# Rotation issued in three steps, and the next batch's normalized sequence in two halves scaled by GpSimd, in a transformer layer on one core

## The chip, the core and the metric

The kernel runs on one core of a Trainium2 chip. The metric is the device time of one execution in microseconds (us), lower is better. The engines are named as the profile names them: PE is TensorE (PEld its weight loads), DVE is VectorE, ACT is ScalarE, POOL is GpSimd, and SP is SyncE, whose queue issues the DMAs of this kernel. Each engine runs its own instructions in the order in which they were issued, and waits for others through semaphores.

## The reference

Four sequences of 1024 tokens with 1024 features, float32. Attention has 32 heads of 32 features, and the feed-forward part sends each token to the best of eight low-rank adapters.

```python
# x: (4, 1024, 1024); layernorm has no weights, eps = 1e-5
x = x + attn(layernorm(x), wq, wk, wv, wo)
x = x + ffn(layernorm(x), route_w, A, Bw)

def attn(x, ...):                        # H, HD = 32, 32
    q, k, v = x @ wq, x @ wk, x @ wv     # each split into heads
    q, k = rotary(q), rotary(k)          # pairs of features: x0*cos - x1*sin, x0*sin + x1*cos
    probs = softmax(causal(q @ k.T / sqrt(HD)))
    return (probs @ v) @ wo

def ffn(x, ...):                         # E, R = 8, 16
    logits = x @ route_w.T               # the best expert, weighted by its logit
    wh = one_hot(argmax(logits)) * max(logits) * (x @ A.T)
    return wh @ Bw                       # summed over experts and ranks
```

## The kernel before

**Units.** The work is cut into 32 units (b, g): four batches b of eight groups g of four heads, whose 4 x 32 features fill the 128 partitions. A unit computes scores, softmax and values for its four heads. The scores come in rounds in the fixed order SLOTS: pieces named by the block t of 64 queries (t = 0 to 15, block t has (t + 1) x 64 keys, so a query row of score data has (t + 1) x 32 elements per partition) are computed in the order 7 and 6; 5, 4 and 3; then "second"; 2, 1, 0 and 9; 15; 14; 13; 12; then "first"; 11 with a part of 8; 10 with the rest. "first" multiplies the probabilities of this unit's first half of the queries by the values, "second" those of the second half of the unit before.

**A round.** `score_round` has PE write the scores into the tile `s` (L381), the only buffer of its PSUM pool; ACT copies them to SBUF (`pr`, L392); POOL adds the causal mask on the diagonal block (L395). `find_tops` has DVE take the row maxima (`top`, L413) and join two partition groups (`both`, L434). Later ACT exponentiates (L442), and DVE transposes (L467). `apply` multiplies with the values (`av`, L548) into the same PSUM tile as the scores, and DVE scales the product by the reciprocal sums and so empties the tile (`scale_values`, L568). The reciprocal sums are spread by a POOL copy (`by`, L512), transposed by PE (L522) and copied by ACT (L523).

**Steps between the rounds.** The rest of the work is a list of `Step` objects for each unit, `between[u]`, each with a cost. After every round `fill` takes steps off the list in order, until their costs reach the round's share of what is left. So the program's order is written once, when it is built, and every step's instructions join their engines' queues at that point. For a unit u the list holds the projections of unit u + 1, by `chain`: q, k and v, each for the two halves `tb` of the sequence, eight matmuls of 128x512 a chain (L295). From batch 1 on it also has the output projection of the batch before, `po` with its streamed weight `chunk` (L665), and that tile's norm, routing and adapter.

**Rotation.** `chain` ends in `finish`. For q and k, ACT copies PSUM to `raw` (L321, L323), DVE shuffles neighbouring partitions into `other` (named swapq or swapk, L325), POOL multiplies `raw` by the cosines in place (L326), DVE multiplies `other` by the signed sines (L327), and POOL adds both into `qT` or `kT` (L328). All five are issued at once. Since L326 writes `raw`, which the shuffle reads, it waits for the shuffle. `raw` and `other` share three buffers of the tag rope.

**The first norm.** Class `Norm` brings the eight tiles of 128 tokens of a batch into `xnT`, the normalized and transposed sequence. `load` reads a tile (L127; some tiles are kept in the next unit's `qT` and `kT`, L246, by the table `homes`). `find` takes moments (`find_moments`: DVE L175, L177 and L179, then POOL raises to the power -0.5, L181). `scale` normalizes in place by one DVE instruction (L186); before it scales tile t it finds the moments of tile t + 1. `turn` transposes by PE in two banks `pt_a` (L198), and copies them to `xnT`, the first bank by ACT (L200), the second by DVE (L204), or by ACT in batch 0. `xnT` is one tile of 128 x 8 x 1024 with one buffer, so no tile of the next batch can be turned before the last v chain of the present batch has read it. `change_steps` and `begin_steps` write the list of steps of the unit in which batches change: the output projection's steps with turnings 0 to 3 among them, then the q and k chains woven with turnings 4 to 7. From batch 0 to 1 there is no output projection, so turnings 0 to 3 stand at the front of the list. The next batch's x tiles share four `row` buffers with the residual tiles; SP issues their loads in order with the weight chunks, the values' round trip through DRAM and the stores.

**Masks behind rotations.** POOL's queue holds masks, rotation products and sums, the powers and the copies of L512, in the order of issue.

Of the kernel before, what the change touches and what calls it, by code (L numbers as in the profile page):

```python
# [9 lines left out]
F32 = mybir.dt.float32  # L10
AF = mybir.ActivationFunctionType
ALU = mybir.AluOpType
AX = mybir.AxisListType

P = 128
# [42 lines left out]
def weave(main, other):  # L58

    if not other:  # L60
        return list(main)
    out, taken = [], 0
    for n, step in enumerate(main):
        out.append(step)
        due = (n + 1) * len(other) // len(main)
        out += other[taken:due]
        taken = due
    return out + list(other[taken:])
# [3 lines left out]
def tile_preln_attn_then_top1_lora(  # L72
# [17 lines left out]
    nc = tc.nc  # L90
# [7 lines left out]
    NC = D // P  # L98
# [6 lines left out]

    const = ctx.enter_context(tc.tile_pool(name="const", bufs=1))
    big = ctx.enter_context(tc.tile_pool(name="big", bufs=1))
    COUNT = {"row": 4, "w": 2, "qkT": 4, "rope": 3, "vT": 1, "vals": 1}
    small = ctx.enter_context(tc.tile_pool(name="small", bufs=2))
    dram = ctx.enter_context(tc.tile_pool(name="dram", bufs=2, space=bass.MemoryType.DRAM))  # L110
    ps_s = ctx.enter_context(tc.tile_pool(name="ps_s", bufs=1, space=bass.MemoryType.PSUM))
# [69 lines left out]
        nc.gpsimd.tensor_tensor(rstd, ve, half_sb, ALU.pow)  # L181
        return mv, rstd

    def normalize(dst, src, moments):
        mv, rstd = moments
        nc.vector.tensor_scalar(dst, src, mv[:, 0:1], rstd, ALU.subtract, ALU.mult)  # L186

    def layernorm(dst, src, name):
        normalize(dst, src, find_moments(src, name))
# [30 lines left out]

    xnTs, qTs, kTs, vTs = {}, {}, {}, {}

    class Norm:


# [28 lines left out]
        def scale(self, t):  # L254
            while self.scaled <= t:
                k = self.scaled
                self.find(k + 1)
                normalize(self.x[k], self.x[k], self.moments.pop(k))
                self.scaled += 1

        def turn(self, t):
            if t == 0:
                xnTs[self.b] = big.tile([P, NC, S], F32, tag="xnT", name=f"xnT_{self.b}")
            self.scale(t)
            dst = xnTs[self.b][:, :, t * P : (t + 1) * P]
            transposed(dst, self.x.pop(t), f"a{self.b}_{t}", scalar_only=not self.b)
            self.load(*self.after.get(t, ()))

        def scaling(self, t):
            return Step(lambda: self.scale(t), 0.0)  # L270

        def turning(self, t):
            return Step(lambda: self.turn(t), 2.0)

        def steps(self, tiles):

# [7 lines left out]
    def chain(u, n, tb, parts=False):  # L284


        b = units[u][0]
        cols = slice(tb * HALF, (tb + 1) * HALF)
        at = {}

        def step(c):
            if c == 0:
                at["p"] = bank([P, HALF], f"p{n}_{u}_{tb}")
            wt = weights[u, n]
            nc.tensor.matmul(  # L295
                at["p"],
                lhsT=wt[:, c, :],
                rhs=xnTs[b][:, c, cols],
                start=(c == 0),
                stop=(c == NC - 1),  # L300
            )
            if c == NC - 1:
                finish()

        def finish():
            if tb == 1:
                weights.pop((u, n))
                if (u, n) != (0, "v"):
                    load_weights()
            if n == "v":  # L310
                if tb == 0:
                    vTs[u] = big.tile([P, S], F32, tag="vT", name=f"vT_{u}")
                nc.scalar.copy(vTs[u][:, cols], at["p"])
                return
            dsts = qTs if n == "q" else kTs
            if u not in dsts:
                dsts[u] = big.tile([P, S], F32, tag="qkT", name=f"{n}T_{u}", bufs=4)
            dst = dsts[u]
            raw = big.tile([P, HALF], F32, tag="rope", name=f"raw{n}_{u}_{tb}", bufs=3)
            if n == "q":  # L320
                nc.scalar.mul(raw, at["p"], scale)  # L321
            else:
                nc.scalar.copy(raw, at["p"])  # L323
            other = big.tile([P, HALF], F32, tag="rope", name=f"swap{n}_{u}_{tb}", bufs=3)
            nc.vector.stream_shuffle(other, raw, SWAP)  # L325
            nc.gpsimd.tensor_tensor(raw, raw, cos_sb[:, cols], ALU.mult)  # L326
            nc.vector.tensor_tensor(other, other, sin_sb[:, cols], ALU.mult)  # L327
            nc.gpsimd.tensor_tensor(dst[:, cols], raw, other, ALU.add)  # L328

        def part(t):  # L330

            if t == 0:
                at["p"] = bank([P, HALF], f"p{n}_{u}_{tb}")
            wt = weights[u, n]
            for c in range(NC):
                nc.tensor.matmul(
                    at["p"][:, t * P : (t + 1) * P],
                    lhsT=wt[:, c, :],
                    rhs=xnTs[b][:, c, t * P : (t + 1) * P],
                    start=(c == 0),  # L340
                    stop=(c == NC - 1),
                )
            if t == TB - 1:
                finish()

        if parts:
            return [Step(lambda t=t: part(t), 2.0) for t in range(TB)]
        return [Step(lambda c=c: step(c)) for c in range(NC)]
# [241 lines left out]

    def load_wo():

        wt = big.tile([P, NC, D], F32, tag="xnT", name="wo_all")
        wo_all.append(wt)
        for n in range(2):
            cols = slice(n * 512, (n + 1) * 512)
            for c in range(NC):
                nc.sync.dma_start(wt[:, c, cols], wo[c * P : (c + 1) * P, cols])

    kept = {}  # L600

# [29 lines left out]
    def finish_steps(b, t, kind="stream"):  # L631
# [22 lines left out]
        def project(n, c, k=None, start=None, stop=None):  # L654
            if c == start:
                st["po"] = bank([P, 512], f"po_{name}_{n}_{start}")
            if k is None:
                rhs = wo_all[0][:, c, n * 512 : (n + 1) * 512]
            else:
                rhs = take_chunk(k)  # L660
            if c < far:
                lhsT = st["at"][:, c, :]
            else:
                lhsT = last_attn[t // TB][:, (t % TB) * P : (t % TB + 1) * P]
            nc.tensor.matmul(st["po"], lhsT=lhsT, rhs=rhs, start=(c == start), stop=(c == stop))  # L665
            if k is not None:
                load_chunk(k + 4)
            if c == stop:
                y = st["y"]
                cols = slice(n * 512, (n + 1) * 512)  # L670
                nc.vector.tensor_tensor(y[:, cols], st["po"], y[:, cols], ALU.add)
                if n == 1 and stop == NC - 1:
                    st["yn"] = kept[t - TB] if last and t >= TB else row(f"yn_{name}")
                    layernorm(st["yn"], y, f"f{name}")
# [85 lines left out]
        return Step(fetch, 0.0), chains, tail  # L760


    def begin_steps(u, norm, project_end):

        q0k0 = chain(u, "q", 0) + chain(u, "k", 0)
        out = [norm.scaling(TB)] + weave(q0k0[:13], norm.steps(range(TB, NT))) + project_end + q0k0[13:]
        for n, tb in (("q", 1), ("k", 1), ("v", 0), ("v", 1)):
            out += chain(u, n, tb)
        return out

    def change_steps(u, norm, project, tail):


        turn, route, turn_hidden, adapt = tail
        p, turning, scaling = project, norm.turning, norm.scaling
        out = [*p[:3], turn, *p[3:5], route, *p[5:8], turn_hidden, *p[8:11], adapt]
        out += [Step(lambda: norm.load(2, 5), 0.0), scaling(1), *p[11:13], turning(0), scaling(2)]
        out += [turning(1), scaling(3), *p[13:15], turning(2), turning(3)]
        return out + begin_steps(u, norm, p[15:])

    norms = {}
    between, late_fetch = [], {}
# [1 line left out]
    for u, (b, g) in enumerate(units):  # L784
# [10 lines left out]


        if u + 1 < len(units) and g + 1 == NG:
            if b:
                homes = {0: "q", 1: "k", 3: "q", 4: "k"}
                norm = Norm(b + 1, {0: (3,), 1: (4,), 2: (6,), 5: (7,)}, homes)  # L800
                steps = change_steps(u + 1, norm, project, tail)
            else:
                norm = Norm(b + 1, {0: (5,), 1: (6,), 2: (7,)}, {4: "k"})
                for t in reversed(range(TB)):
                    between[-1].insert(16 + 8 * t, norm.scaling(t))
                between[-1].insert(0, Step(lambda norm=norm: norm.load(*range(TB)), 0.0))
                steps = [norm.turning(t) for t in range(TB)] + begin_steps(u + 1, norm, [])
            norms[b + 1] = norm
        else:
            steps = []  # L810
# [74 lines left out]
    def do(s):  # L885
        if s.chunk:
            s.run(numbers[s])
        else:
            s.run()

    for s in start:
        do(s)
# [43 lines left out]
    second, first_ = SLOTS.index("second"), SLOTS.index("first")  # L936
    final = len(units) - 1
    for u, (b, g) in enumerate(units):
        todo.extend(between[u])
        ends_at = n_slots  # L940
        if b + 1 < B and g + 1 == NG:
            norms[b + 1].load(*((0, 1) if b else (TB,)))
        if u == final:
            load_wo()
            ends_at = second
# [121 lines left out]
```

## Time and profile before

| | |
|---|---|
| median of the three runs | 2840.68 us (2840.13, 2840.68, 2847.22) |
| the profiled execution | 2841.66 us |
| its span, first to last instruction | 2839.9 us |
| mean granted clock of PE | 0.983 |
| row maxima, L413, DVE | 652.1 us in 768 instructions |
| causal masks, L395, POOL | 238.5 us in 512 instructions |
| rotation products of k, L326, POOL | 114.1 us in 64 instructions |
| normalization of one tile, L186, DVE | 0.80 us, up to 1.50 |
| second copy of a turned tile, DVE L204 / ACT L200 | 0.69 / 0.59 us |

Busy times come from one profiled execution. In a row of the timeline the columns are start, busy time, engine, line, operation, output and inputs, tile and number of instructions, and in brackets the idle time of the engine before it and what ended that. A count such as x5 means that neighbouring instructions of one kind are drawn together, with the tile of one of them. In a row of the windows each engine's busy us in the stretch is followed by its number of instructions; then come PE's granted clock, the busy share of the DMA engines and GB/s. In a row of the waits the numbers are the us in total, how often, and the longest.

### The profile page before, as it was taken

How to read it: one execution, taken by the hardware profiler on the slowest of the kernel's cores; microseconds unless marked ns; L12 is line 12 of the kernel's file. 1: busy time of each engine (PE TensorE's matmuls, PEld its weight loads, DVE VectorE, ACT ScalarE, POOL GpSimd, SP SyncE). 2: the span in 40 equal slices, each digit the busy share in tenths (PEclk: the TensorE clock that was granted, in tenths of full speed). 3: DMA queues.
4: the chain of work that ended last, by engine and by line, in shares of the span. 5: the costliest groups of instructions: out<-in, count | busy, mean ns of one | idle time of the engine just before them, and what ended most of it. 6: DMA issues, size and time to landing. Idle time of an engine off the chain costs nothing.

```text
span 2839.9 us, 84110 instructions
## 1 busy us (share of the span) xinstructions
PE 2713.1 (96%) x35328; PEld 1334.1 (47%) x35328; DVE 2119.5 (75%) x4225; ACT 1746.1 (61%) x5006; POOL 711.7 (25%) x900
## 2 busy tenths in 40 slices
PE   8999999889999999988999999998999999999998
PEld 5444444344444444443445544444444445444445
DVE  4777777887777777787777787777777777877655
ACT  2776777676667666655666666664666666676421
POOL 2322222323222222212222222221222222222000
PEclk9999999999999999999999999999999999999999
DMA  3222222223544544562454445545164444445521
GB/s 114 50 54 54 54 51 51 82 72 85 141 125 134 143 133 127 135 191 50 117 157 117 122 124 145 140 128 177 46 168 121 139 124 115 127 135 146 168 65 53
DMA packets 448011, 317.86 MB, mean 112 GB/s; under 512 B 150288, under 2 KB 371728, under 8 KB 447632
## 3 DMA queue, kind: packets, MB, share of 16 engines
q1 hardware_dynamic: 447632, 312.47, 40.0%
q8 instruction: 278, 4.55, 0.7%
q14 instruction: 101, 0.83, 0.1%
HBM read 262.59 MB, written 49.81 MB: 110 GB/s over the span
## 4 chain that ended last, share of the span: by engine, by line
PE 81%; DVE 10%; POOL 3%; DMA 2%; ACT 2%; issue 1%; SPq 0%; POOLq 0%; DVEq 0%; ACTq 0%
PE po L665 14%; PE pq L295 14%; PE pv L295 13%; PE pk L295 13%; PE s L381 12%; PE av L548 8%; DVE top L413 4%; DVE pr L467 2%; PE ph L686 2%; PE pf L725 2%; PE pr L522 1%; DVE both L434 1%; DMA chunk<-in_wo 1%; PE pt_f L198 1%; POOL pr L395 1%
## 5 line engine op out<-in xcount | busy, mean ns | idle before, releaser
L442 ACT ACTIVATE pr<-pr,both 128x256 f32<-128x256 f32 (+15 forms) x2048 | 1047.1, 520 | 40.4 <-DVE both L434 39.6
L413 DVE TENSOR_REDUCE top<-pr 128x2 f32<-128x960 f32 (+15 forms) x768 | 652.1, 896 | 354.4 <-POOL pr L395 353.1
L392 ACT COPY pr<-s 128x640 f32<-128x640 f32 (+14 forms) x544 | 525.9, 1018 | 563.5 <-PE s L381 563.3
L467 DVE STREAM_TRANSPOSE pr<-pr 128x1024 f32<-128x1024 f32 (+11 forms) x768 | 671.4, 910 | 51.2 <-ACT pr L442 47.3
L395 POOL TENSOR_TENSOR pr<-pr,causal_sb 128x128 f32<-128x128 f32 x512 | 238.5, 472 | 1054.2 <-ACT pr L392 1045.4
L295 PE MATMUL pv<-xnT,wv 128*128 128x512 f32 x1024 | 489.5, 607 | 0.0
L295 PE MATMUL pq<-xnT,wq 128*128 128x512 f32 x1008 | 483.3, 607 | 3.2 <-ACT xnT L200 3.2
L295 PE MATMUL pk<-xnT,wk 128*128 128x512 f32 x1008 | 474.8, 601 | 1.5 <-ACT rawq L321 1.5
L381 PE MATMUL s<-kT,qT 32*32 32x256 f32 (+4 forms) x17408 | 403.3, 395 | 48.7 <-DVE at L568 47.1
L442 ACT ACTIVATION_READ_ACCUMULATOR pr<-pr,both 128x1 f32 x2048 | 402.6, 197 | 0.0
L665 PE MATMUL po<-chunk,attn 128*128 128x512 f32 x736 | 377.5, 600 | 7.2 <-DMA chunk<-in_wo 7.2
L381 PEld LDWEIGHTS s<-kT,qT 32*32 32x32 f32 x17408 | 190.9, 104 | 306.9 <-issue 174.8
L295 PEld LDWEIGHTS pv<-xnT,wv 128*128 128x128 f32 x1024 | 189.1, 193 | 223.8 <-issue 219.0
L295 PEld LDWEIGHTS pq<-xnT,wq 128*128 128x128 f32 x1008 | 184.8, 193 | 232.5 <-issue 228.1
L295 PEld LDWEIGHTS pk<-xnT,wk 128*128 128x128 f32 x1008 | 182.1, 190 | 236.9 <-issue 234.0
L548 PE MATMUL av<-pr,vals 64*32 64x256 f32 (+3 forms) x12288 | 269.2, 318 | 4.2 <-issue 2.1
L548 PEld LDWEIGHTS av<-pr,vals 64*32 64x32 f32 x12288 | 212.2, 105 | 110.7 <-issue 28.7
L665 PEld LDWEIGHTS po<-chunk,attn 128*128 128x128 f32 x736 | 135.1, 190 | 174.7 <-issue 150.7
L434 DVE TENSOR_TENSOR both<-top 32x4 f32<-32x4 f32 (+3 forms) x1152 | 187.3, 163 | 23.7
L523 ACT COPY by<-pr 128x512 f32<-128x512 f32 x64 | 37.5, 586 | 260.8 <-PE pr L522 260.8
L326 POOL TENSOR_TENSOR rawk<-rawk,cos_sb 128x512 f32<-128x512 f32 x64 | 114.1, 1784 | 289.0 <-DVE swapk L325 289.0
L326 POOL TENSOR_TENSOR rawq<-rawq,cos_sb 128x512 f32<-128x512 f32 x64 | 114.1, 1782 | 246.4 <-DVE swapq L325 246.4
(88 smaller groups left out, 1723.8 us busy)
## 6 DMA issues: line engine op xcount, KB each, us to landing
chunk<-in_wo SPq DMA_DIRECT2D x368, 256.0 KB, 3.8
vals<-vd SPq DMA_DIRECT2D x256, 128.0 KB, 4.4
x<-in_x SPq DMA_DIRECT2D x55, 512.0 KB, 5.8
wq<-in_wq SPq DMA_DIRECT2D x32, 512.0 KB, 4.1
wk<-in_wk SPq DMA_DIRECT2D x32, 512.0 KB, 4.2
wv<-in_wv SPq DMA_DIRECT2D x32, 512.0 KB, 4.2
vd<-vT SPq DMA_DIRECT2D x128, 128.0 KB, 4.8
out_y<-x SPq DMA_DIRECT2D x32, 512.0 KB, 2.8
```

The lines of the kernel that those rows point to most:

```text
L295: nc.tensor.matmul(at["p"], lhsT=wt[:, c, :], rhs=xnTs[b][:, c, cols], start=(c == 0), stop=(c == NC - 1),)
L326: nc.gpsimd.tensor_tensor(raw, raw, cos_sb[:, cols], ALU.mult)
L381: nc.tensor.matmul(sc[i * SQ : (i + 1) * SQ, h, at : at + w].rearrange("p (j k) -> p j k", k=SQ), lhsT=of_q[rows, 2 * t + half], rhs=of_k[ ...
L392: nc.scalar.copy(pr[:, :, k0 : k0 + w], sc[:, :, at : at + w])
L395: nc.gpsimd.tensor_tensor(diagonal, diagonal, causal_sb.unsqueeze(1).to_broadcast([P, HG, SQ]), ALU.add)
L413: nc.vector.tensor_reduce(top[:, k, h : h + step], places[u, t][:, h : h + step, :], AX.X, ALU.max, negate=True,)
L434: nc.vector.tensor_tensor(dst[rows], src[rows], src[other], op)
L442: nc.scalar.activation(pr[:, h, :], pr[:, h, :], AF.Exp, bias=tops[u, t][:, h : h + 1], accum_out=dens[u, t // QT][:, t % QT, h : h + 1],)
L467: nc.vector.transpose(pr, pr)
L548: nc.tensor.matmul(avs[half][h * HD : (h + 1) * HD, t0:, :], lhsT=v[rows, j, h * HD : (h + 1) * HD], rhs=rhs, start=(j == 0), stop=(j == n ...
L665: nc.tensor.matmul(st["po"], lhsT=lhsT, rhs=rhs, start=(c == start), stop=(c == stop))
L686: nc.tensor.matmul(ph, lhsT=st["ynT"][:, c, :], rhs=w[:, c - i * RA, :], start=(c == 0), stop=(c == NC - 1),)
```

## The change

1. The rotation is taken apart. `finish` makes only the raw copy. A list `postponed` with `do_postponed` runs after every step and counts its cost: after two units of cost the shuffle, the product (which now writes `qT` or `kT` and leaves `raw` alone) and the sine product are issued, after two more the sum, now in place in `qT` or `kT`. Whatever is left is issued at the start of a unit.
2. `xnT` becomes two halves of 128 x 8 x 512 in two buffers. The first half's buffer is free after the last v chain of that half. Turnings of the next batch's first tiles (0 to 3 from batch 0 to 1, tile 0 in the later changes) move among the last steps of the list before, that is among the last v chain, and the output weights for the last batch are two tiles for the same reason.
3. In batches 1 to 3 `normalize` runs on POOL, two `tensor_scalar` of 128x512 for a tile in place of one of 128x1024 on DVE (48 in place of 24), and both copies of a turned tile are ACT's in all batches (24 ACT copies in place of 24 on DVE). A turning costs 1.3 instead of 2.0 in the lists of batches 1 to 3.
4. The tag row has five buffers instead of four, x tiles are loaded earlier and in other homes, and `change_steps` sets another order of chains and turnings, in the change from batch 0 too; `begin_steps` is gone.

```diff
--- before.py
+++ after.py
...
     big = ctx.enter_context(tc.tile_pool(name="big", bufs=1))
-    COUNT = {"row": 4, "w": 2, "qkT": 4, "rope": 3, "vT": 1, "vals": 1}
+    COUNT = {"row": 5, "w": 2, "qkT": 4, "rope": 3, "vT": 1, "vals": 1}
     small = ctx.enter_context(tc.tile_pool(name="small", bufs=2))
...
 
-    def normalize(dst, src, moments):
+    def normalize(dst, src, moments, engine=None):
         mv, rstd = moments
-        nc.vector.tensor_scalar(dst, src, mv[:, 0:1], rstd, ALU.subtract, ALU.mult)
+        if engine is None:
+            nc.vector.tensor_scalar(dst, src, mv[:, 0:1], rstd, ALU.subtract, ALU.mult)
+            return
+        for n in range(D // 512):
+            cols = slice(n * 512, (n + 1) * 512)
+            engine.tensor_scalar(dst[:, cols], src[:, cols], mv[:, 0:1], rstd, ALU.subtract, ALU.mult)
 
...
 
+
+    postponed = []
+
+    def do_postponed(cost):
+        for item in list(postponed):
+            item[0] -= cost
+            if item[0] <= 0:
+                postponed.remove(item)
+                item[1]()
+
     class Norm:
...
                 self.find(k + 1)
-                normalize(self.x[k], self.x[k], self.moments.pop(k))
+                engine = nc.gpsimd if self.b else None
+                normalize(self.x[k], self.x[k], self.moments.pop(k), engine)
                 self.scaled += 1
 
         def turn(self, t):
-            if t == 0:
-                xnTs[self.b] = big.tile([P, NC, S], F32, tag="xnT", name=f"xnT_{self.b}")
+            half, k = divmod(t, TB)
+            if k == 0:
+                xnTs[self.b, half] = big.tile(
+                    [P, NC, HALF], F32, tag="xnT", name=f"xnT_{self.b}_{half}", bufs=2
+                )
             self.scale(t)
-            dst = xnTs[self.b][:, :, t * P : (t + 1) * P]
-            transposed(dst, self.x.pop(t), f"a{self.b}_{t}", scalar_only=not self.b)
+            dst = xnTs[self.b, half][:, :, k * P : (k + 1) * P]
+            transposed(dst, self.x.pop(t), f"a{self.b}_{t}", scalar_only=True)
             self.load(*self.after.get(t, ()))
 
         def scaling(self, t):
             return Step(lambda: self.scale(t), 0.0)
 
         def turning(self, t):
-            return Step(lambda: self.turn(t), 2.0)
+            return Step(lambda: self.turn(t), 2.0 if self.b == 0 else 1.3)
 
...
                 lhsT=wt[:, c, :],
-                rhs=xnTs[b][:, c, cols],
+                rhs=xnTs[b, tb][:, c, :],
                 start=(c == 0),
...
                 nc.scalar.copy(raw, at["p"])
-            other = big.tile([P, HALF], F32, tag="rope", name=f"swap{n}_{u}_{tb}", bufs=3)
-            nc.vector.stream_shuffle(other, raw, SWAP)
-            nc.gpsimd.tensor_tensor(raw, raw, cos_sb[:, cols], ALU.mult)
-            nc.vector.tensor_tensor(other, other, sin_sb[:, cols], ALU.mult)
-            nc.gpsimd.tensor_tensor(dst[:, cols], raw, other, ALU.add)
+
+            def turn():
+                other = big.tile([P, HALF], F32, tag="rope", name=f"swap{n}_{u}_{tb}", bufs=3)
+                nc.vector.stream_shuffle(other, raw, SWAP)
+                nc.gpsimd.tensor_tensor(dst[:, cols], raw, cos_sb[:, cols], ALU.mult)
+                nc.vector.tensor_tensor(other, other, sin_sb[:, cols], ALU.mult)
+                postponed.append([2.0, lambda: add(other)])
+
+            def add(other):
+                nc.gpsimd.tensor_tensor(dst[:, cols], dst[:, cols], other, ALU.add)
+
+            postponed.append([2.0, turn])
 
...
 
-    def begin_steps(u, norm, project_end):
-
-        q0k0 = chain(u, "q", 0) + chain(u, "k", 0)
-        out = [norm.scaling(TB)] + weave(q0k0[:13], norm.steps(range(TB, NT))) + project_end + q0k0[13:]
-        for n, tb in (("q", 1), ("k", 1), ("v", 0), ("v", 1)):
-            out += chain(u, n, tb)
-        return out
-
     def change_steps(u, norm, project, tail):
 
 
-        turn, route, turn_hidden, adapt = tail
         p, turning, scaling = project, norm.turning, norm.scaling
-        out = [*p[:3], turn, *p[3:5], route, *p[5:8], turn_hidden, *p[8:11], adapt]
-        out += [Step(lambda: norm.load(2, 5), 0.0), scaling(1), *p[11:13], turning(0), scaling(2)]
-        out += [turning(1), scaling(3), *p[13:15], turning(2), turning(3)]
-        return out + begin_steps(u, norm, p[15:])
+        out, chains = [], []
+        for n, tb in (("q", 0), ("k", 0), ("q", 1), ("k", 1), ("v", 0), ("v", 1)):
+            chains += chain(u, n, tb)
+        if p:
+            turn, route, turn_hidden, adapt = tail
+            out += [*p[:2], scaling(1), turn, *p[2:4], turning(1), route, scaling(2), *p[4:6], turning(2)]
+            out += [turn_hidden, scaling(3), p[6], adapt, Step(lambda: norm.load(7), 0.0)]
+            out += [turning(3), scaling(4), p[7]]
+            chains = weave(chains[:-6], p[8:]) + chains[-6:]
+        else:
+            out += [scaling(4)]
+        for t, n in zip(range(TB, NT), (3, 4, 5, 4)):
+            out += chains[:n] + [turning(t)] + [scaling(t + 1)] * (t + 1 < NT)
+            del chains[:n]
+        return out + chains
 
...
         if u + 1 < len(units) and g + 1 == NG:
+            last_v = between[-1]
             if b:
-                homes = {0: "q", 1: "k", 3: "q", 4: "k"}
-                norm = Norm(b + 1, {0: (3,), 1: (4,), 2: (6,), 5: (7,)}, homes)
-                steps = change_steps(u + 1, norm, project, tail)
+                norm = Norm(b + 1, {0: (1,), 1: (4,), 2: (5,), 3: (6,)}, {2: "q", 3: "k", 5: "q", 6: "k"})
+                last_v.insert(len(last_v) - 6, norm.turning(0))
+                last_v.insert(len(last_v) - 15, norm.scaling(0))
+                last_v.insert(len(last_v) - 24, Step(lambda norm=norm: norm.load(0), 0.0))
             else:
-                norm = Norm(b + 1, {0: (5,), 1: (6,), 2: (7,)}, {4: "k"})
+                norm = Norm(b + 1, {0: (5,), 1: (6,), 2: (7,)})
                 for t in reversed(range(TB)):
-                    between[-1].insert(16 + 8 * t, norm.scaling(t))
-                between[-1].insert(0, Step(lambda norm=norm: norm.load(*range(TB)), 0.0))
-                steps = [norm.turning(t) for t in range(TB)] + begin_steps(u + 1, norm, [])
+                    last_v.insert(len(last_v) - 7 + 2 * t, norm.turning(t))
+                for t in reversed(range(TB)):
+                    last_v.insert(12 + 7 * t, norm.scaling(t))
+                last_v.insert(0, Step(lambda norm=norm: norm.load(*range(TB + 1)), 0.0))
+            steps = change_steps(u + 1, norm, project, tail)
             norms[b + 1] = norm
...
             s.run()
+        do_postponed(s.cost)
 
...
     for u, (b, g) in enumerate(units):
+        do_postponed(math.inf)
+        do_postponed(math.inf)
         todo.extend(between[u])
         ends_at = n_slots
         if b + 1 < B and g + 1 == NG:
-            norms[b + 1].load(*((0, 1) if b else (TB,)))
+            if b:
+                norms[b + 1].load(2, 3)
         if u == final:
```

More of the change, by code (lines that the diff above doesn't have):

```diff
@@ L338, in part @@
                     lhsT=wt[:, c, :],
-                    rhs=xnTs[b][:, c, t * P : (t + 1) * P],
+                    rhs=xnTs[b, tb][:, c, t * P : (t + 1) * P],
                     start=(c == 0),
@@ L591, in load_wo @@
     def load_wo():
-        wt = big.tile([P, NC, D], F32, tag="xnT", name="wo_all")
-        wo_all.append(wt)
         for n in range(2):
             cols = slice(n * 512, (n + 1) * 512)
+            wt = big.tile([P, NC, 512], F32, tag="xnT", name=f"wo_{n}", bufs=2)
+            wo_all.append(wt)
             for c in range(NC):
-                nc.sync.dma_start(wt[:, c, cols], wo[c * P : (c + 1) * P, cols])
+                nc.sync.dma_start(wt[:, c, :], wo[c * P : (c + 1) * P, cols])
     kept = {}
@@ L657, in project @@
             if k is None:
-                rhs = wo_all[0][:, c, n * 512 : (n + 1) * 512]
+                rhs = wo_all[n][:, c, :]
             else:
```

## The prediction

> **What bounds the kernel now.** I read the page's first part, then the chain that ended last, then a table of windows, then TensorE's (PE's) waits, and last the timeline of one repeated unit of work. From the page:
>
> ```profile
> span 2839.9 us, 84110 instructions
> PE 2713.1 (96%) x35328; PEld 1334.1 (47%) x35328; DVE 2119.5 (75%) x4225; ACT 1746.1 (61%) x5006; POOL 711.7 (25%) x900
> ...
> PE 81%; DVE 10%; POOL 3%; DMA 2%; ACT 2%; issue 1%; SPq 0%; POOLq 0%; DVEq 0%; ACTq 0%
> ```
>
> PE is busy for 96%, so only 127 us of the span can be idle. The change takes no matmul away; it can win only that idle time and the cold clock after it. The windows (us, then busy us by engine, then granted clock) show where it is:
>
> ```profile
> 351.00:423.00 72.00, 65.87 (x1034) 31.14 (x1032) 56.73 (x112) 53.04 (x155) 20.54 (x26) 0.95 0.22 53
> 495.00:576.00 81.00, 67.70 (x1055) 32.38 (x1065) 67.30 (x133) 53.32 (x156) 23.96 (x30) 0.92 0.27 73
> 576.00:662.00 86.00, 76.27 (x1128) 39.26 (x1097) 71.67 (x141) 57.82 (x164) 24.03 (x30) 0.94 0.25 69
> 801.00:890.00 89.00, 89.00 (x1236) 44.35 (x1236) 69.70 (x140) 56.91 (x164) 24.54 (x29) 1.00 0.46 128
> 1239.00:1308.00 69.00, 49.58 (x680) 26.71 (x679) 53.39 (x112) 30.54 (x102) 14.74 (x20) 0.94 0.57 158
> ```
>
> A unit inside batches 1 to 3 (801) has PE full at clock 1.00. A unit of batch 0 (351) lacks 6 us, the two units around the change from batch 0 to 1 (495, 576) 13 and 10, and a later change of batch (1239) 19. PE's waits say on what:
>
> ```profile
> PE s L381 <- DVE at L568: 47.1, 8, 11.2
> PE pt_a L198 <- DVE x L186: 29.1, 7, 9.3
> PE pt_a L198 <- DVE kT L186: 7.2, 2, 3.9
> PE pt_a L198 <- DVE qT L186: 6.9, 4, 2.3
> ```
>
> The first is a score round that waits for VectorE (DVE) to empty the shared PSUM tile (L568); the others are transposes of a tile of x that wait for its normalization. The timeline of one batch-0 unit (start, us, engine, operation, idle before and its releaser) shows how DVE comes to be late:
>
> ```profile
> 377.31 1.79 POOL L326 TENSOR_TENSOR rawk<-rawk,cos_sb 128x512 f32<-128x512 f32 x1 [6.70 <-DVE swapk L325]
> 379.18 1.27 POOL L328 TENSOR_TENSOR kT<-rawk,swapk 128x512 f32<-128x512 f32 x1
> 380.42 1.70 POOL L395 TENSOR_TENSOR pr<-pr,causal_sb 128x128 f32<-128x128 f32 x4
> 380.90 2.80 DVE L413 TENSOR_REDUCE top<-pr 128x4 f32<-128x384 f32 x5 [1.32 <-POOL pr L395]
> 389.11 1.79 POOL L326 TENSOR_TENSOR rawq<-rawq,cos_sb 128x512 f32<-128x512 f32 x1 [4.54 <-DVE swapq L325]
> 390.98 1.28 POOL L328 TENSOR_TENSOR qT<-rawq,swapq 128x512 f32<-128x512 f32 x1
> 392.21 0.46 POOL L395 TENSOR_TENSOR pr<-pr,causal_sb 128x128 f32<-128x128 f32 x1
> 392.71 2.21 DVE L413 TENSOR_REDUCE top<-pr 128x2 f32<-128x960 f32 x2 [2.13 <-POOL pr L395]
> 412.65 2.37 PE L381 MATMUL s<-kT,qT 32*32 32x384 f32 x64 [6.13 <-DVE at L568]
> ```
>
> GpSimd (POOL) runs in order: a rotation's product waits for DVE's shuffle, its sum follows, and the causal masks queue behind both; the row maxima (top) wait for the masks; after further DVE work stands L568, for which PE waits 6.13 us.
>
> **Rotation apart, in batch 0.** The shuffle moves some steps behind the raw copy, the product writes qT or kT and so no longer waits for the shuffle, and the sum comes a step later. No instruction is added. I follow a unit by the rows: the score copy of round 14 ended at 390.31, so its mask could end at about 390.8 if the sum did not stand in front (the product, 1.79, can start at 387.7, when the raw copy ends). Top 14 then starts when DVE is free, at 390.9 instead of 392.71: 1.8 us earlier. Reciprocal, its copy, mask 13 and top 13 move with it (397.9 for 399.73). At round 12 the score copy ended at 400.07 and the mask stood at 406.48, behind product and sum; top 12 now starts when DVE is free, which takes out its wait of 0.66. The wait of 1.32 at 380.90 goes as well, but the changed order puts shuffle and sine product (0.74 + 0.69 = 1.43) behind those tops, and the sum of the first k half (1.27) now stands ahead of mask 15: a new wait, with top 15 and DVE's whole queue behind it, which eats what was won there. So L568 ends 1.8 + 0.7 = 2.5 us earlier and the wait of 6.13 becomes 3.6. What is late next is L568 still. Six units have this wait (3.63 once, the others 5.5 to 6.1, 33.5 us together): 6 x 2.5 = 15. The round after such a wait took 2.37 us, also after the wait of 3.63, but 1.48 after one of 2.37; the next matmuls show the same, some 1.5 us in all. Only the unit with 3.63 gets under that: +1.5. Term: 17 us, bounds 8 to 26.
>
> In units like 801 PE is full, and L568 ends 1.2 to 1.6 us before its round. The same new wait costs at most 1.27 there, so I take 0; without that cover it would be up to 21 units x 1.3 = 27 us.
>
> **Change 0 to 1.** Waits now: 11.24 before a score round, then 2.06, 1.63, 1.95, 2.94, 0.83 and 2.37, together 23.0, and 3 us twice of matmuls at the low clock: 29. The halves of the normalized sequence let four transposed tiles (1.04 us of PE each) move ahead among the last v steps: 4.2 us fill the 11.24. Four scalings of 0.80 to 1.50 leave DVE there, two of them (1.50 + 1.48) ahead of L568. Of 11.24, some 4 stay. The copies that the transposes waited for all go to ACT (0.59 each for DVE's 0.69), busy only 53 of 81 us; the waits 1.63, 1.95, 2.94 and 0.83 lie where tiles now arrive a unit early. I leave 10 to 11 of the 29: term 18, bounds 8 to 24.
>
> **Changes 1 to 2 and 2 to 3.** Waits now 19.4 (2.93, 0.50, 2.18, 1.37, 2.25, 3.33, 0.76, 6.11) and 19.6. Scaling goes from one DVE instruction of 0.80 to two of POOL by 128x512. No such row exists: POOL's copy of that size took 0.61, its two-input sum 1.27 and product 1.78. A scaling streams one tensor, so the copy is nearest: 0.9 each, 1.8 a tile, bounds 1.2 to 3.6. Statistics stay on DVE (1.28 + 0.21 + 0.15), the power on POOL (0.55 to 0.98). A tile on the path thus costs about 1.0 more than now. By the changed order the second and third tile still wait on PE, about 6.4 and 8.7 us, since the statistics of the tile after them are issued first, and tiles 3, 6 and 7 for 0.6, 2.8 and 0.8: 19.3, nothing won. Counted by DVE's work instead (8 x 0.80 and 8 copies x 0.69 leave a stretch in which it is busy 53 of 69) up to 8 are won. I take 3.5 each: 7, bounds -20 (every scaling at the product's 1.78 and masks behind it) to +16. The x loads (landing 5.8 us) are issued earlier on SP's queue, ahead of weight chunks; waits for chunks are 7.2 us in all, so I give that -1 to +3, and with a start whose wait of 2.33 may go, a fifth row buffer and the output weights in halves: +1 together.
>
> The Trainium skill, "GPSIMD Engine Reference", sections 3.1 and 4.1, speaks against the scaling's move: elementwise work belongs on VectorE, GpSimd being about twice as slow with two inputs and roughly at line rate with one; its best loop of 1.8 cycles an element would make an estimated 0.77 us a piece, below my 0.9; taken at the two-input rate of 2.6 cycles, an estimated 1.11, the sum would lose about 5 us more over 24 late pieces.
>
> A second cost is in the rows: DVE's normalize takes 0.80 alone and 1.50 at 539.13, while POOL multiplies, and POOL's power 0.55 or 0.98. With the scalings on POOL, the two-input DVE operations near them may stretch POOL likewise; that is inside the bound 3.6.
>
> The same page, section 1, says that the two share SBUF interfaces when VectorE runs in a two-port mode or reads two inputs from SBUF; by it, moving work between them would free less time than the 0.80 rows promise; the third term would then go to 0 and the time to 2805.
>
> **Sum.** The profiled execution took 2841.66 us (span 2839.9). 17 + 18 + 7 + 1 = 43 gives 2798.7; the median of the runs is 1.0 lower, so 2798. Half-widths 9, 8, 18 and 2, taken as independent, make 22: 2776 to 2820 for this case.
>
> **Rivals.**
> - *POOL becomes the bound at the changes of batch* (slower). 48 pieces stand in POOL's queue ahead of masks, with tops and PE behind. If every piece lies on the path, the gain of 43 is used up at 0.9 + 43/48 = 1.8 us a piece, and at 2.0 it is 0.3% slower; at 2.2 the time is 2798 + 62 = 2860. For it: the product's 1.78. Against: the sum's 1.27 although it reads two tensors, and tiles 0, 3, 4 and 5 have matmuls beside them. 0.13.
> - *The rotation wins nothing*: the new wait ahead of mask 15 passes on to all tops. Batch 0 stays: 2798 + 17 = 2815. For it: DVE is busy 57 of 72 and its queue almost closed after 392. 0.15.
> - *The batch-0 waits close wholly*, the clock with them: 33.5 + 6 x 1.5 = 42 for 17: 2773. Against it: DVE's own work of 57 us has no slack between top 12 and L568. 0.12.
> - My forecast: 0.60.
>
> A measurement of this kernel can tell about 0.3% (8.5 us) from no change. Below 2832 lie nearly all of my case, and the second and third rival: 0.82; within 2832 to 2849 a poor outcome of the POOL term: 0.05; above, the first rival: 0.13. The range 2768 to 2835 leaves out the first rival and the far ends, under 0.2.
>
> **What would show it.** In the profile after: waits of s on L568's successor of about 3.6 us in six units of batch 0 (0 to 1 would be the third rival, 6 the second); before 0 to 1 one of about 4 and none on x copies behind; at the later changes pt_a waiting for POOL instead of DVE, about 19 us each; GpSimd scalings at 0.9 us; no wait of s on DVE in the full units. Scalings above 1.8 us, or idle PE in units like the one at 801, would prove the sum wrong.

## The result, and the profile after

The changed kernel is slower: median 2857.03 us of 7 runs (2853.74 to 2860.14) against 2840.74 us, a ratio of 1.0052 with a 95% interval of 1.0039 to 1.0065. The forecast was 2798. The first lines of the page (span; busy time of the engines; the chain that ended last) show PE with the same matmuls, and POOL more on the chain, with a new line L191, the scaling (L407, L594, L203 and L187 here are L381, L568, L198 and L186 of the kernel before):

```profile
span 2855.7 us, 84162 instructions
PE 2723.4 (95%) x35328; PEld 1341.7 (47%) x35328; DVE 2115.2 (74%) x4177; ACT 1755.0 (61%) x5030; POOL 738.6 (26%) x948
...
PE 79%; DVE 12%; POOL 4%; issue 2%; ACT 2%; DMA 0%; SPq 0%; POOLq 0%; DVEq 0%; ACTq 0%
PE po L691 14%; PE pq L314 13%; PE pk L314 12%; PE pv L314 12%; PE s L407 11%; PE av L574 8%; DVE top L439 4%; DVE pr L493 3%; PE ph L712 2%; PE pf L751 2%; POOL x L191 2%; DVE both L460 1%; PE pr L548 1%; ACT pr L418 1%; PE pt_f L203 1%
```

Where the time went is read from the start of the score round on block 15 in each unit, in both profiles. Units are counted from 0. The round of unit 5 starts 12.4 us earlier than before, that of unit 8 only 3.5 earlier: the change from batch 0 to 1 cost 8.8. The change 1 to 2 cost 9.7 more, 2 to 3 10.9; full units take 82.33 us in both kernels.

The windows (columns as before; the unit ahead of the change 0 to 1, and the change 1 to 2) show POOL busy 37 of 88 and 41 of 83 us. PE's waits, in the second block, show on what PE stood still:

```profile
482.00:570.00 88.00, 73.87 (x1064) 38.59 (x1064) 62.83 (x131) 54.52 (x156) 37.06 (x39) 0.88 0.32 91
1237.00:1320.00 83.00, 56.00 (x679) 30.27 (x678) 41.09 (x89) 33.57 (x107) 41.00 (x34) 0.79 0.38 106
```

```profile
PE s L407 <- DVE at L594: 34.5, 8, 7.0
PE pt_a L203 <- POOL x L191: 32.0, 11, 8.0
PE pt_a L203 <- POOL qT L191: 21.4, 5, 9.7
PE pt_a L203 <- DVE x L187: 10.0, 2, 9.3
PE pt_a L203 <- POOL kT L191: 9.6, 4, 3.8
PE av L574 <- ACT pr L418: 6.4, 1, 6.4
```

The waits of `s` on DVE fell from 47.1 to 34.5 us; PE now waits 63 us for POOL's scalings, 26.4 of them at the change 1 to 2, where it waited 15.2 for tiles before, and its granted clock there is 0.79. One group of instructions (ns: least, median, greatest) gives the price:

```profile
L191 POOL TENSOR_SCALAR x<-x,mv_a,rstd_a x32: 2067/2074/2587, 505.8 to 2012.8; 128x512 f32<-128x512 f32 x32
```

A piece takes 2.07 us, a tile 4.13 to 4.15 in the timeline. What that does to the queue is seen ahead of the change from batch 0 to 1 (timeline of POOL and DVE, with rows left out between those shown):

```profile
518.88 4.13 POOL L191 TENSOR_SCALAR x<-x,mv_a,rstd_a 128x512 f32<-128x512 f32 x2
522.98 0.46 POOL L421 TENSOR_TENSOR pr<-pr,causal_sb 128x128 f32<-128x128 f32 x1
523.47 2.35 DVE L439 TENSOR_REDUCE top<-pr 128x2 f32<-128x1024 f32 x2 [4.61 <-POOL pr L421]
...
530.27 4.13 POOL L191 TENSOR_SCALAR x<-x,mv_a,rstd_a 128x512 f32<-128x512 f32 x2
534.37 1.26 POOL L352 TENSOR_TENSOR qT<-qT,swapq 128x512 f32<-128x512 f32 x1
535.59 0.46 POOL L421 TENSOR_TENSOR pr<-pr,causal_sb 128x128 f32<-128x128 f32 x1
536.08 2.21 DVE L439 TENSOR_REDUCE top<-pr 128x2 f32<-128x960 f32 x2 [5.63 <-POOL pr L421]
```

Each mask stands behind a scaling (the second behind a rotation's sum too), and the row maxima wait 4.61 and 5.63 us for the masks. PE then waits 6.38 us ahead of the values (`av`). The wait of the next score round, 6.97, is not shown to come from POOL: it was 11.24 before, and with the scaling back on DVE (below) it is 8.79, while the wait of `av` is gone.

### The profile page after: what moved, and what is told of

Read it like the earlier page. It is cut to its first block, busy times and chain, and to the rows that moved or that the text cites. A ratio compares the mean times of both kernels' runs of the same rounds, so it can differ in the third digit from the quotient of the medians.

```text
span 2855.7 us, 84162 instructions
## 1 busy us (share of the span) xinstructions
PE 2723.4 (95%) x35328; PEld 1341.7 (47%) x35328; DVE 2115.2 (74%) x4177; ACT 1755.0 (61%) x5030; POOL 738.6 (26%) x948
## 4 chain that ended last, share of the span: by engine, by line
PE 79%; DVE 12%; POOL 4%; issue 2%; ACT 2%; DMA 0%; SPq 0%; POOLq 0%; DVEq 0%; ACTq 0%
PE po L691 14%; PE pq L314 13%; PE pk L314 12%; PE pv L314 12%; PE s L407 11%; PE av L574 8%; DVE top L439 4%; DVE pr L493 3%; PE ph L712 2%; PE pf L751 2%; POOL x L191 2%; DVE both L460 1%; PE pr L548 1%; ACT pr L418 1%; PE pt_f L203 1%
## 5 line engine op out<-in xcount | busy, mean ns | idle before, releaser
L407 PE MATMUL s<-kT,qT 32*32 32x256 f32 (+4 forms) x17408 | 403.2, 395 | 35.2 <-DVE at L594 34.5
L407 PEld LDWEIGHTS s<-kT,qT 32*32 32x32 f32 x17408 | 190.2, 104 | 293.7 <-issue 149.5
L460 DVE TENSOR_TENSOR both<-top 32x4 f32<-32x4 f32 (+3 forms) x1152 | 214.5, 186 | 23.6
L352 POOL TENSOR_TENSOR kT<-kT,swapk 128x512 f32<-128x512 f32 x64 | 81.5, 1273 | 166.0 <-DVE swapk L348 165.8
L352 POOL TENSOR_TENSOR qT<-qT,swapq 128x512 f32<-128x512 f32 x64 | 81.5, 1273 | 138.4 <-DVE swapq L348 138.2
```

The costliest lines, as they stand in the source:

```text
L352: nc.gpsimd.tensor_tensor(dst[:, cols], dst[:, cols], other, ALU.add)
L407: nc.tensor.matmul(sc[i * SQ : (i + 1) * SQ, h, at : at + w].rearrange("p (j k) -> p j k", k=SQ), lhsT=of_q[rows, 2 * t + half], rhs=of_k[ ...
L460: nc.vector.tensor_tensor(dst[rows], src[rows], src[other], op)
```

## The experiments

Theory S: the scaling's price on POOL is the loss, the rest of the change brings about what was forecast. Rival O: the new order of turnings and the copies on ACT are the loss. Ratios are to the kernel before, with 95% intervals.

| kernel | median us | ratio |
|---|---|---|
| changed, scaling on DVE | 2817.39 | 0.9912 (0.9895 to 0.9929) |
| before, rotation in three steps | 2825.91 | 0.9941 (0.9926 to 0.9956) |
| before, scaling on POOL | 2890.48 | 1.0168 (1.0150 to 1.0187) |
| before, short POOL forms at the end | 2842.82 | one run |
| changed, scaling on ACT | 2791.46 | 0.9825 (0.9812 to 0.9838) |
| changed, DVE, scaling ahead of the next statistics | 2810.17 | 0.9889 (0.9875 to 0.9902) |
| changed, DVE, second copy on DVE | 2822.24 | 0.9933 (0.9921 to 0.9946) |
| changed, DVE, turnings ahead of the round | 2816.85 | 0.9912 (0.9899 to 0.9926) |
| before, scaling on ACT | 2837.84 | 0.9991 (0.9980 to 1.0002) |
| changed, POOL in four pieces | 2865.84 | 1.0087 (1.0072 to 1.0101) |
| before, product writes qT or kT | 2823.90 | 0.9940 (0.9927 to 0.9953) |
| changed, ACT, product writes qT or kT, all at once | 2791.47 | 0.9819 (0.9803 to 0.9835) |

**Scaling back on DVE.**

```diff
-                engine = nc.gpsimd if self.b else None
+                engine = None
```

> The changed kernel with one edit: the normalization of batches 1 to 3 is back on DVE (24 instructions of 128x1024 in place of 48 on POOL). Theory S (the scaling alone is the loss: its pieces took 2.07 us each where 0.9 was assumed, 4.15 a tile, and stand ahead of masks and transposes): the rest of the change brings what was forecast, so 2795 us, between 2785 and 2810; in units 6 and 7 the idle PE falls by some 20 us, the waits of pt_a at the two later changes from 26 us each to 10 to 15. Rival O (the new order of turnings and chains, which puts a tile's statistics only just ahead of its use, and all copies on ACT, are the loss): 2840 to 2855, pt_a waits for DVE as long as it waited for POOL.

Measured 2817.39: 40 us of the changed kernel's time are the choice of engine. S holds for the cause, but 2795 was not reached: the rest is worth 25, not 43. Units 6 and 7 are 15 us shorter than with POOL. PE's waits on tiles at the change 1 to 2 are now 16.8 us, more than S expected. Over the whole run its waits on normalized tiles are

```profile
PE pt_a L203 <- DVE x L187: 31.2, 7, 9.1
PE pt_a L203 <- DVE qT L187: 15.5, 2, 7.8
PE pt_a L203 <- DVE kT L187: 2.7, 2, 1.3
```

together 49.4 us, where the four `pt_a` rows of the changed kernel make 73.0. So by PE's waits the larger part of POOL's price, some 24 us, came straight through the tiles, and 6.4 through the masks (`av`).

**Rotation alone, on the kernel before.** The edit is the rotation's part of the diff.

> The kernel before with the rotation in three steps alone. Theory S: batch 0 wins what it won in the changed kernel, 12.4 us up to the start of its sixth unit, and about 2 more in units 6 and 7: 2841 - 14 = 2827, between 2822 and 2832; the six waits of the score round on DVE are 3.9 us instead of 6.1. Rival: the win in batch 0 came from the earlier loads, the halves or the copies, not from the rotation: 2838 to 2843, waits of 6.1.

Measured 2825.91, 15 to 17 us better, and the six waits add up to 22.6 us (3.4 to 3.9 each) where they were 33.5. The round at the change 0 to 1 waits 8.7 instead of 11.2.

**Scaling on POOL alone, on the kernel before.** With `normalize` in two pieces as in the diff:

```diff
-                normalize(self.x[k], self.x[k], self.moments.pop(k))
+                engine = nc.gpsimd if self.b else None
+                normalize(self.x[k], self.x[k], self.moments.pop(k), engine)
```

> The kernel before with the scaling of batches 1 to 3 on POOL alone. Theory S: a tile's scaling takes 4.15 instead of 0.80 us on the way to PE; of 24 tiles some 12 to 18 are waited for, so +40 to +60 us: 2880 to 2900. Rival O: DVE is relieved by as much as POOL is loaded, and the price is small, 2845 to 2855.

Measured 2890.48, 48 us slower: S. In the profile the three changes cost 16.0, 18.8 and 17.5 us more than before.

**The price by itself.** Nine instructions behind the last step: `tensor_scalar` with two scalars per partition at three widths, with one, with two constants, with one; a copy; `tensor_tensor` with a broadcast operand, and with two whole ones.

> The kernel before with ten short POOL instructions added behind the last step, on constants that nothing uses any more: the disputed cost by itself. If the 2.07 us are a price for each element and each of the two operations, the pieces take 1.05, 2.07 and 4.1 us for 256, 512 and 1024 columns, and one operation half of it; if they are the price of the scalars read per partition, the form with two constants takes about 0.9 and with one 0.6, like the copy of 0.61; if they are a start cost, all three widths take nearly 2 us. Time of the whole: about 10 us over the kernel before.

The groups of that run (busy us, mean ns):

```profile
L1021 POOL TENSOR_SCALAR sin_sb<-cos_sb,half_sb,sign_sb 128x1024 f32<-128x1024 f32 x1 | 3.8, 3779 | 0.1
...
L1021 POOL TENSOR_SCALAR sin_sb<-cos_sb,half_sb,sign_sb 128x512 f32<-128x512 f32 x1 | 2.1, 2072 | 0.1
L1023 POOL TENSOR_SCALAR sin_sb<-cos_sb 128x512 f32<-128x512 f32 x1 | 1.9, 1932 | 0.1
L1022 POOL TENSOR_SCALAR sin_sb<-cos_sb,sign_sb 128x512 f32<-128x512 f32 x1 | 1.6, 1571 | 0.1
L1024 POOL TENSOR_SCALAR sin_sb<-cos_sb 128x512 f32<-128x512 f32 x1 | 1.5, 1497 | 0.1
L1021 POOL TENSOR_SCALAR sin_sb<-cos_sb,half_sb,sign_sb 128x256 f32<-128x256 f32 x1 | 1.3, 1337 | 0.0
L1027 POOL TENSOR_TENSOR sin_sb<-sin_sb,cos_sb 128x512 f32<-128x512 f32 x1 | 1.3, 1267 | 0.1
L1026 POOL TENSOR_TENSOR sin_sb<-cos_sb,sign_sb 128x512 f32<-128x512 f32 x1 | 1.0, 1038 | 0.1
L1025 POOL COPY sin_sb<-cos_sb 128x512 f32<-128x512 f32 x1 | 0.6, 609 | 0.1
```

The two-scalar form takes 2072 ns here too, but DVE still works beside it (the nine instructions run from 2820.1 to 2835.9 of 2841.0 us), so this run alone doesn't rule out contention. The trace of the changed kernel does: 24 of its 48 pieces had no DVE instruction beside them and took 2.07 to 2.08 us, as the others did, but for three of 2.59 and 2.62. It is the form's own price. It grows with the columns (1337, 2072 and 3779 for 256, 512 and 1024), scalars per partition cost only 0.14 us over constants, and one operation takes 1.5, not half of two. So none of the three guesses is right as it stood: the form itself is dear, with one input dearer than a product of two tensors. The expected 10 us over the kernel before didn't come either, since POOL had idle time beside the last steps.

**Scaling on ACT, in the changed order.** One instruction instead of POOL's two, its bias made by a short one:

```diff
+            nc.vector.tensor_scalar(less, mv[:, 0:1], -1.0, None, ALU.mult)
...
+            nc.scalar.mul(mv, mv, rstd)
+            nc.scalar.activation(dst, src, AF.Identity, bias=mv, scale=rstd)
```

> As the changed kernel, but a tile of batches 1 to 3 is normalized by ACT in one instruction of 128x1024 (x times the power plus a bias), with 0.15 us on DVE and a short ACT instruction to make the bias. Question: would the forecast's larger terms at the changes of batch have come if the scaling had left DVE for an engine that does it at a small price? Theory P (yes, DVE is the bound there and 0.80 a tile matters): 2805 to 2812, below the 2817 of DVE scaling, the wait of 8.8 us before the score round near 6. Rival (ACT's own queue of exponentials stands ahead of the tile as POOL's masks did): 2820 to 2830.

Measured 2791.46, better than P expected, some 50 us under the kernel before, and the wait before the round at 0 to 1 is 7.3, not 6. An instruction takes 1.24 us and its bias 0.3, nearly twice DVE's 0.80, and still wins 26 us over DVE. PE's waits on tiles in its profile:

```profile
PE pt_a L211 <- ACT x L192: 14.1, 5, 4.5
PE pt_a L211 <- DVE x L195: 9.8, 2, 9.1
PE pt_a L211 <- ACT qT L192: 4.3, 2, 2.5
```

26 us are more than the 24 x 0.80 = 19 of work that left DVE, so P's reason is not the whole. The place in the queue counts as well: at the change 1 to 2 the third tile's scaling stood on DVE behind row maxima and the statistics of the tile after it (1235.61 to 1240.20), and PE waited 7.69 us; on ACT it starts at 1233.19, and PE waits 1.82.

**Scaling ahead of the next tile's statistics, on DVE.** `self.find(k + 1)` is called behind `normalize` in batches 1 to 3.

> The changed kernel with DVE scaling, and a tile's normalization issued ahead of the next tile's statistics instead of behind them, in batches 1 to 3. Theory Q (the long waits of pt_a, 4.8 and 7.7 us at each later change, contain the next tile's statistics, 1.65 us each): the waits fall to about 3 and 6, total -6 to -10: 2807 to 2811. Rival: DVE then stands still for POOL's power (0.55 to 0.98) at every tile and wins nothing: 2815 to 2820.

Measured 2810.17; the starts of units show the two later changes shorter by 2.0 and 4.4 us. At the change 1 to 2 the two long waits fell from 4.75 and 7.69 to 3.87 and 6.18. Q explains a part of those waits.

**Second copy back on DVE.** `scalar_only=not self.b`.

> The changed kernel with DVE scaling, and the second copy of a turned tile back on DVE in batches 1 to 3 (24 copies of 0.69 us for 24 of ACT of 0.59). Theory S (DVE is the bound at the changes): slower by 24 x 0.69 x some half: 2822 to 2828. Rival O (all copies on ACT are part of the shortfall): 2805 to 2813.

Measured 2822.24, 5 us slower by the medians, as S expected; the intervals just overlap.

**Turnings ahead of the waiting round.** The four steps at the change 0 to 1 get cost 0 and stand behind the last step of v's first half.

> The changed kernel with DVE scaling, and the four transposed tiles of the change from batch 0 to 1 all ahead of the score round that waits for DVE, where the forecast had put them (three of the four stand behind it in the changed kernel). Theory R (that is where the forecast's term of 18 went): the wait of 8.8 falls by about 2 to 3 us and the units 6 and 7 together get 3 to 5 us shorter: 2812 to 2815. Rival (the wait is DVE's whole queue, and PE's work before or behind it changes nothing): 2817, units 6 and 7 as before.

Measured 2816.85, no gain. The wait before the round went, but a transpose ahead of it now waits 7.46 us for ACT. So PE's work moved there doesn't shorten the change: what it needs next, a copy by ACT, is late too.

**Scaling on ACT, in the order before.**

> The kernel before, with only the scaling of batches 1 to 3 moved to ACT (as in the kernel that took 2791 us). It completes the table of two orders and three engines. Theory P (at the changes DVE's queue is the bound in either order, and 0.80 a tile off it is worth about as much as in the new order, 26 us): 2815 to 2825. Rival (the gain needs the new order, in which tiles are turned while PE has other steps): 2832 to 2842.

Measured 2837.84, an interval that holds no change: the rival. What wins 26 us in the new order is worth at most some 6 in the old one.

**POOL's pieces made dearer.** `D // 256` pieces of 128x256 instead of `D // 512` of 128x512.

> The changed kernel with each tile's scaling on POOL in four pieces of 128x256 instead of two of 128x512: the suspected price made larger and nothing else. By the row measured for 256 columns a tile takes 4 x 1.34 = 5.35 instead of 4.15 us, 1.2 more, 29 us over 24 tiles. Theory S (POOL's time for a scaling stands on PE's path): 14 to 29 us slower than the changed kernel, 2871 to 2886, by the share of the tiles that are waited for. Rival O (the loss is the order, and POOL's time is mostly covered): 2857 to 2862.

Measured 2865.84. In a row the pieces took 1.22 each, 4.9 a tile, so 0.75 more over 24 tiles is 18 us, not 29, and 8.8 arrived: about half, between what S and O had put. The same half comes from the engine: 3.35 more a tile than DVE is 80 us, 40 arrived.

**The rotation's product alone.**

```diff
-            nc.gpsimd.tensor_tensor(raw, raw, cos_sb[:, cols], ALU.mult)
+            nc.gpsimd.tensor_tensor(dst[:, cols], raw, cos_sb[:, cols], ALU.mult)
...
-            nc.gpsimd.tensor_tensor(dst[:, cols], raw, other, ALU.add)
+            nc.gpsimd.tensor_tensor(dst[:, cols], dst[:, cols], other, ALU.add)
```

> The kernel before, with the rotation issued all at once as there, and only this of the change: the product writes qT or kT, so it doesn't wait for the shuffle any more. Which part of the rotation's change brings its 17 us? If it is the wait of the product, then most of it: in the unit of the prediction top 14 starts 1.1 instead of 1.8 us earlier and top 12's wait of 0.66 goes, so the six waits of the score round fall from 6.1 to about 4.4: 2841 - 12 = 2829, between 2825 and 2833. If it is the later issue of shuffle and sum, 2836 to 2842, waits near 6.

Measured 2823.90, even a little under the expected range and level with the rotation in three steps. The waits are 4.6 instead of 3.9 us (3.2 in the first unit), yet the time is the same: by the starts of units it wins 9.0 up to unit 5, where three steps won 12.2, and makes that up at the changes of batch. The edit takes out two costs at once, which no run parts: the wait for the shuffle, and the length of the product, 1.78 before and 1.28 now.

**Both findings together.** The changed order, ACT, the product's edit, no postponing.

> The kernel that took 2791 us (changed order, scaling on ACT), with the rotation issued all at once again and only its product writing qT or kT. If the product's wait was the whole cost of the rotation here too, 2788 to 2796, no slower than with the three steps; if the later issue of shuffle and sum matters once the changes of batch are shorter, 2798 to 2806.

Measured 2791.47: level. It is with the other ACT kernel the fastest here, and needs no `postponed` list.

## Why the prediction was wrong

**The step that failed** is the price of a scaling: "A scaling streams one tensor, so the copy is nearest: 0.9 each, 1.8 a tile, bounds 1.2 to 3.6." It took 2.07 a piece and 4.13 a tile, above the upper bound. The bound was wrong in kind: the rows of before held only POOL copies and two-tensor operations, and I took the number of streamed tensors for what sets the price. In the prediction's sum this is "A tile on the path thus costs about 1.0 more than now": it was 3.35 more. The first rival had the engine and the place right, though the masks and tops that it named carried less than the tiles themselves (6.4 and some 24 us of PE's waits); it was given 0.13 because the price was thought bounded, and the range stopped short of it. Its formula gives 2798 + 48 x 1.17 = 2854, near the measured 2857, but in part by chance: only half of POOL's extra time reached the path, and without it the changed kernel stands at 2817, not 2798.

**Rotation (forecast 17).** The size was right, 15 to 17 alone, but not all where I put it: the six waits lost 10.9 us and units 6 and 7 about 4.8 more in the profiles. The waits became 3.9 for the forecast 3.6, and the first unit's 3.63 stayed, so its clock gain did not come. The new wait of the sum ahead of mask 15 cost full units nothing. And the reason was half right: the product's edit alone brings the whole gain, so the in-place write, which held the product until the shuffle was done, was the cost, and postponing adds nothing to the total that these runs can tell. That the product itself would become 0.5 us shorter was not foreseen.

**Change 0 to 1 (forecast 18).** By the starts of units 5 to 8 it lost 8.8 us with POOL, won 6.3 with DVE, of which the rotation alone makes 4.8, and 9.6 with ACT. Two steps were mis-sized besides the price: transposes were to fill the wait of 11.24, but three of the four stand behind that round, and moving them ahead wins nothing; and new waits came in (5.8 us on the fifth tile, on DVE).

**Changes 1 to 2 and 2 to 3 (forecast 3.5 each).** -9.7 and -10.9 with POOL, +3.0 and +1.1 with DVE, +15.5 and +13.5 with ACT. With the scaling on ACT the gain forecast for these two changes would have been too small. Why the old order wins nothing from ACT is not shown by a run of its own; in the profile of that kernel PE waits for ACT in two new places, 7.1 us for the raw copies of q and 4.7 for score copies.

**The rest (forecast 1), and the other rivals.** The round on block 15 of unit 0 starts at 85.06 instead of 85.74 us: 0.7 won at the start. PE's waits for weight chunks fell from 7.2 to 0.4, more than the -1 to +3 that was given them; but 6.1 of the 7.2 lie at the two later changes, inside the 19.4 and 19.6 of the term before. No run takes this term by itself, so its size stays open. The second rival (the rotation wins nothing) and the third (its waits close wholly) are both out by the waits of 3.9 us.

One reading of a row was wrong as well: at 539.13 POOL was not multiplying but adding (the rotation's sum, 538.81 to 540.09), and it was that sum beside which DVE's normalization took 1.50. The stretch that the prediction allowed for on POOL came for three of the 48 pieces.

The Trainium skill, "GPSIMD Engine Reference", section 4.1, was right in its direction (elementwise work belongs on VectorE: 0.80 us a tile there, 4.15 on POOL). Its figure of section 3.1 for a good loop, 0.77 us for 512 elements, is not what `tensor_scalar` takes here: 2.07.

## What to carry to other kernels

Before work moves to another engine, look for a row of the very instruction there; where none exists, the bound has to reach above the dearest row (here 1.78, and the price was 2.07), or a run must measure it first. Adding up an instruction's own time isn't enough either, since each engine works in order: about half of the time added on POOL reached the end, and on ACT more was won than the time that left DVE. Ask what stands ahead of each moved instruction in its queue, and what behind. And when a chain is postponed to get rid of a wait, look first for the buffer that makes it wait: writing to another tile brought the whole gain of a scheduling change.

## What the runs showed of the hardware

On POOL a `tensor_scalar` of 128x512 takes 1.50 us with one constant and 2.07 with two scalars per partition, where a product with a broadcast operand takes 1.04 and one of two tensors 1.27. By the pieces of 1.22 (in a row), 2.07 and 3.78 us for 256, 512 and 1024 columns, 256 columns with two scalars cost 0.85 us and each instruction an estimated 0.37 besides.

A product on POOL and one on DVE that both read two tensors get in each other's way, and the one that begins second pays. In the kernel before all 128 rotation products began 0.05 us after DVE's sine product of 0.69 and took 1.77 to 1.80 us. Where only the product's target was changed, 109 of 128 no longer met it and took 1.26 to 1.30. Eighteen began ahead of it and kept 1.27 or 1.28, and the sine product took 0.98 to 1.51, ending 0.55 us after the product each time; one began behind and took 1.74. The Trainium skill, "GPSIMD Engine Reference", section 1, names such a shared access; its size here is 0.5 us.

ACT's normalization of 128x1024 took 1.24 us.
